# The gated recurrence issued step by step among the chunks of the masked cross attention

## The chip, the cores and the metric

The kernel runs on one core of one Trainium2 chip. The metric is the device time of one execution in microseconds (us). Before the change three runs took 3279.47, 3282.17 and 3289.09 us; the median is 3282.17 us. A difference of 0.3% is about 10 us. Five engines work side by side, each taking its own instructions in the order in which they were issued: PE (matrix products and transposes, with PEld as its weight loads), DVE (vector operations), ACT (activation functions and copies), POOL (elementwise work beside DVE, and the gathers) and SP (which issues most DMAs). The results of PE go to PSUM, here eight buffers ("banks") of 128 x 512 numbers.

## The reference

A decoder of four blocks on 128 sequences of 64 tokens with 128 features. Each of its twelve steps is `x = layernorm(x + step(x))`: attention of some kind, cross attention to a context, and a feed-forward step. The three steps that matter here stand at the end of the third block and the beginning of the fourth:

- `L2_ffn`: a short convolution, a mixture of eight experts, an RMS norm, and a small feed-forward step;
- `L3_attn`: no attention in the usual sense, but a gated recurrence. With `xn` the RMS-normed input, `q, kv, a = split(xn @ W.T)`, the state is `h[t] = sigmoid(a[t]) * h[t-1] + kv[t]`, and the output is `q * h`;
- `L3_xattn`: cross attention with 16 heads of 8 features under a mask that differs for every sequence, query and key.

After them comes `L3_ffn`, a routed mixture of experts (top 1).

## The kernel before

The 8192 tokens are 16 chunks `X[0]` to `X[15]` of 512 tokens (`CT`; 8 sequences), each held in SBUF as 128 partitions x 4 x 128 numbers for the whole run. A list `steps` calls one function per step; the loads of the next step's weights and the functions follow each other, and a scheduler inside the framework fixes the order of instructions on each engine from the program's order and its own estimate of times. `tc.issue_after(ins)` adds an edge of issue order: what is issued inside must stand behind `ins` on its engine.

Buffers come from pools by tag. SBUF tags with their buffer counts are in `SPACES` (`xT`, `qT`, `kT`, `o`, `oT`, `tmp` two each, `r` three). PSUM has `bank()` (three banks) and `wide()` (five banks).

`ffn_conv` works on pairs of chunks in 8 turns. A turn runs eight `units` (one per 128 tokens: expert products, SiLU, weighting, sums), and between them `take` draws steps from two generators: `begin` of the next pair and `end` of the last pair. `end` turns the sums, projects them, computes an RMS norm (`norm`), scales the accumulators (the loop on `h[:, t, :]`), transposes them (`transposed`, L325), and runs the small feed-forward step (products `dn`, a GELU, products `u`). The last pair's `end` runs by itself after the eighth turn, then a last layer norm.

`attn_scan` is the recurrence. For each chunk: squares on ACT, their sum and a reciprocal square root on DVE (`rsqrt`, eleven small dependent operations, L340 to L345), scaling to `xn` half on POOL and half on ACT, four transposes, three products of 512 columns (q, kv, gate), a sigmoid on ACT, the scan on DVE (L1807), a product with q, four transposes back, the residual sum, and the layer norm of the result. It runs as a software pipeline in which chunk i is normed while chunk i-4 gets its layer norm. No other step's work stands beside it, except where one step's end meets the next one's beginning.

`xattn_masked` calls `mha`, the loop that all attention steps share. One iteration c of it holds, in program order: `weights(c, 0)` (products `t_ps` in four wide banks, then four exponentials `e`), the load and transposes of chunk c+2, `values(c-1, 1)`, `scores(c+1, 0)` (products `s_ps` in four wide banks, then four maxima L1183 on DVE), the output transposes of chunk c-1, `project_v(c+1)`, `weights(c, 1)`, `values(c, 0)`, `scores(c+1, 1)`, `project(c+2)` with the eight head-masked copies `eb`, the output product, `maxima(c+1)` (a transpose `mT_ps` on PE and its copy `mT`, L1202) and the layer norm of chunk c-1. The loop goes from c = -2 to 16. A callback `aside(c, k, seen)` is called four times in each iteration, k = 0 to 3, with instructions behind which its work shall stand; `xattn_masked` passes `kept`, which from c = 2 on draws steps of the next step's routing.

The layer norm of a chunk ends on POOL in `ln_apply` (L380, four operations) up to chunk 11, and on ACT (L378) beyond.

Of the kernel before, what the change touches and what calls it, by code (L numbers as in the profile page):

```python
# [12 lines left out]
F32 = mybir.dt.float32  # L13
# [4 lines left out]
ALU = mybir.AluOpType  # L18
# [216 lines left out]
def tile_decoder(ctx: ExitStack, tc: tile.TileContext, a, out):  # L235
# [1245 lines left out]
    def xattn_masked():  # L1481
        w = W[10]

        rows_of = a["amask"], a["amaskT"]
        store = {}
        begin = cross(w, "l3xbq", "l3xbk")

        used = BPC * 8 * 18

        def prepare(c, s):  # L1490
            m = work("t1", (P, BPC * 2 * S // 4), "mu").bitcast(U8), VX[c % 2][:, used + 512 : used + 768].bitcast(U8)
            for x, src in zip(m, rows_of):
                for g in range(4):
                    nc.sync.dma_start(out=x[32 * g : 32 * g + 32], in_=src[c])
            then = begin(c, s)

            def step(n):
                f = (work("ye", (P, 512), "mf") if n == 0 else VX[c % 2][:, used : used + 512]).bitcast(BF16)
                V.tensor_scalar(f, m[n], 0.0, NEG, ALU.is_equal, ALU.mult)
                store[c, n] = f.rearrange("p (b n k) -> p b n k", b=BPC, n=2)  # L1500
                return then(n)

            return step

        def mask(c, hf, s, t):
            for h in range(2):
                for x in range(2):
                    for g in range(4):
                        if s:
                            f = rows32(store[c, 0], g)[:, 4 * hf + x : 4 * hf + 4 : 2, h, None, :].to_broadcast([32, 2, 4, S])  # L1510
                            mm(
                                s[g][x * S : (x + 1) * S].rearrange("p (u h k) -> p u h k", u=2, h=4), rows32(idh, g)[:, h, :], f,
                                start=False, stop=(h == 1), skip_group_check=True,
                            )
                            continue
                        f = rows32(store[c, 1], g)[:, None, 4 * hf : 4 * hf + 4, h, :].to_broadcast([32, 2, 4, S])
                        mm(t[g][x * S : (x + 1) * S], rows32(idh, g)[:, h, :], f, start=False, stop=False, skip_group_check=True)

        mha(
            prepare, w[:, 2, :],  # L1520
            lambda c, s: out_projected(c, s["o"], w[:, 3, :], bv=col("l3xbv"), base=lambda: with_bias(c, "l3xbo"), on_act=c > 11),
            mask=mask, aside=kept,
        )


# [76 lines left out]
    def ffn_conv():  # L1602
# [83 lines left out]
        def end(i):  # L1686
# [27 lines left out]
            for n in pair:  # L1714
                h = acc[n]
                for t in range(TPC):
                    V.scalar_tensor_tensor(h[:, t, :], h[:, t, :], y[:, 0, n, t : t + 1], row("normw"), ALU.mult, ALU.mult)  # L1717
                hT.append(transposed(h, "oT"))
                b = with_bias(2 * i + n, "upb")
                G.tensor_tensor(b, b, h, ALU.add)  # L1720
                base.append(b)
                yield
# [27 lines left out]
        def take(it, n=1):  # L1750
            for _ in range(n):
                next(it, None)
# [5 lines left out]
        for i in range(turns):  # L1758
            b = begin(i + 1) if i + 1 < turns else none
            e = end(i - 1) if i else none  # L1760
            for g in range(8):
                units(i, g // TPC, g % TPC)
                if g == 0:
                    take(tail)
                    take(b, 2)
                elif g == 1:
                    take(e, 2)
                elif g == 2:
                    take(b, 2)
                elif g == 3:  # L1770
                    take(e, 3)
                elif g == 4:
                    take(b, 2)
                elif g == 5:
                    take(b)
                elif g == 6:
                    take(e, 2)
                elif g == 7:
                    take(e)
            tail = e  # L1780
        take(tail)
        for _ in end(turns - 1):
            pass
        v = sm.tile([P, 2, 2, TPC], F32, tag="cv", name="cv")
        G.memset(v[:, 0], 1.0)
        norm(v, turns - 1, S_[turns - 1])
# [1 line left out]


    def attn_scan():  # L1790
        w = W[9]
        xs, hs, rs = {}, {}, {}
        kept = work("h", (P, 8, 512), "scan")

        def project(c):
            xT = transposed(xs.pop(c), "xT", scale=col("gamma"))
            q = bank("q_ps")
            mm(q, w[:, 0, :], xT, start=True, stop=True)
            ps = [wide("kva_ps") for _ in range(2)]
            for k in range(2):  # L1800
                mm(ps[1 - k], w[:, 2 - k, :], xT, start=True, stop=True)
            g = work("qT", name="gate")
            A.activation(g, ps[1], AF.Sigmoid)

            G.memset(g.rearrange("p (b s) -> p b s", b=BPC)[:, :, 0:1], 0.0)
            h = hs[c] = kept[:, c % 8]
            V.tensor_tensor_scan(h, g, ps[0], 0.0, ALU.mult, ALU.add)  # L1807
            V.tensor_tensor(h, h, q, ALU.mult)

        def recalled(c):  # L1810
            h = hs.pop(c)
            y = bank("y")
            for t in range(TPC):
                q = slice(t * P, (t + 1) * P)
                nc.tensor.transpose(y[:, q], h[:, q], ident)
            r = rs[c] = work("r", (P, TPC, D))
            V.tensor_tensor(r, y.rearrange("p (t d) -> p t d", t=TPC), X[c], ALU.add)

        def squares(c):
            s = xs[c] = work("tmp", (P, TPC, D), "sq")  # L1820
            A.activation(s, X[c], AF.Square)


        squares(0)
        for i in range(NC + 4):
            v = sm.tile([P, 2, TPC], F32, tag="lnv2", name="lnv2")
            a_, b_ = i, i - 4
            if a_ < NC:
                V.tensor_reduce(v[:, 0], xs[a_], AX.X, ALU.add)
                V.tensor_scalar(v[:, 0], v[:, 0], 1e-24, None, ALU.max)  # L1830
            else:
                G.memset(v[:, 0], 1.0)
            if b_ >= 0:
                r = rs.pop(b_)
                mv = ln_stats(r, v[:, 1])
            else:
                G.memset(v[:, 1], 1.0)
            if a_ + 1 < NC:
                squares(a_ + 1)
            y = rsqrt(v.rearrange("p n t -> p (n t)"), 2 * TPC, "rms")  # L1840
            if a_ < NC:
                V.tensor_scalar(y[:, :TPC], y[:, :TPC], math.sqrt(D), None, ALU.mult)
                xn = xs[a_] = work("o", (P, TPC, D), "xn")
                for t in range(TPC):
                    if t % 2:
                        A.activation(xn[:, t, :], X[a_][:, t, :], AF.Identity, scale=y[:, t : t + 1])
                    else:
                        G.tensor_scalar(xn[:, t, :], X[a_][:, t, :], y[:, t : t + 1], None, ALU.mult)
            if b_ >= 0:
                ln_apply(b_, r, mv, y[:, TPC:], on_act=True)  # L1850
            if 0 <= i - 3 < NC:
                recalled(i - 3)
            if 0 <= i - 1 < NC:
                project(i - 1)


    n_rows = [(len(cs) * CT + E8 * (GR - 1)) // GR * GR for cs in SWITCH_BATCHES]
# [25 lines left out]
    def ffn_switch():  # L1883
# [5 lines left out]

    steps = [  # L1890
        moe_top2, xattn_single, ffn_ternary, attn_diff, xattn_causal, ffn_routed,
        attn_alibi, xattn_padded, ffn_conv, attn_scan, xattn_masked, ffn_switch,
    ]
    seen = None
    for n, step in enumerate(steps):
        load_weights(n + 1)

        with tc.issue_after(seen) if seen else nullcontext():
            seen = step()
# [16 lines left out]
```

## Time and profile before

| | us |
|---|---|
| median of three runs | 3282.17 |
| the profiled execution | 3278.03 |
| its span on the core | 3276.3 |
| the conv's last turn ends (last `units` on DVE) | 2545 |
| first product of the recurrence (q) | 2586 |
| first transposes of the masked attention | 2689.7 |
| its first `weights` (L1213) | 2710.1 |
| one iteration of its loop (start of `scores` to the next) | 18.95 |

In the page, part 1 gives the busy time of each engine, part 2 the same in 40 slices of some 82 us each. A table of windows gives the busy time in stated stretches, and the timeline lists instructions in order of time: start, duration, engine, line, operation, output from input, count, and in square brackets the idle time before it with what ended it. Where several instructions are merged in one line, the duration is that of the whole group.

### The profile page before, as it was taken

The numbers are of one execution on the slowest core, as the hardware profiler recorded it, in microseconds if no ns is written. First come the engines' busy times: TensorE is split into PE (matmuls) and PEld (weight loads), VectorE is DVE, ScalarE is ACT, GpSimd is POOL, SyncE is SP. The second block draws the span as 40 slices with busy tenths as digits, with TensorE's granted clock in tenths as the row PEclk, the third lists the DMA queues.
The fourth block names the chain that finished last, engine by engine and source line by source line (L and its number), as shares of the span: only waits on it lengthen the run. The fifth ranks groups of instructions, "written<-read, shape, count | busy, mean of one in ns | idle before, by whom it ended". The sixth has DMA issues, their size and how long they took to land. (4 is left out here: it accounts for less than half of the span.)

```text
span 3276.3 us, 110323 instructions
## 1 busy us (share of the span) xinstructions
PE 2882.3 (88%) x47184; PEld 2115.1 (65%) x47184; DVE 1973.2 (60%) x7074; ACT 1614.1 (49%) x3106; POOL 1521.4 (46%) x1548
## 2 busy tenths in 40 slices
PE   5999967999987999999999989998888569998993
PEld 3888834666665777766677767774444336776793
DVE  3733267557777666433256656666778886666246
ACT  3544457445543565333355545643444555654553
POOL 4477473454555344311234445556566322446154
PEclk9999988999998999999999989989988789998997
DMA  5578710000002000000000000000000000001684
GB/s 142 160 214 248 220 52 28 8 1 3 3 3 76 19 4 4 6 1 1 5 11 4 4 5 4 4 13 1 1 1 2 9 1 16 18 15 46 181 266 147
DMA packets 142459, 159.23 MB, mean 49 GB/s; under 512 B 16720, under 2 KB 118096, under 8 KB 141968
## 3 DMA queue, kind: packets, MB, share of 16 engines
q1 hardware_dynamic: 128064, 123.65, 12.7%
q0 software_dynamic: 13184, 27.03, 3.2%
q8 instruction: 370, 6.06, 0.7%
q10 hardware_dynamic: 720, 1.50, 0.1%
q14 instruction: 121, 0.99, 0.1%
HBM read 121.44 MB, written 30.67 MB: 46 GB/s over the span
## 5 line engine op out<-in xcount | busy, mean ns | idle before, releaser
L1183 DVE TENSOR_REDUCE m<-s_ps 128x8 f32<-128x512 f32 x640 | 397.5, 683 | 144.4 <-PE s_ps L1411 50.8
L1232 ACT ACTIVATE e<-t_ps 128x512 f32<-128x512 f32 x640 | 330.0, 601 | 150.7 <-PE t_ps L1225 150.2
L380 POOL TENSOR_SCALAR x<-xb,lnmv,ln_y 128x128 f32<-128x128 f32 x304 | 238.6, 797 | 267.5 <-DVE ln_y L345 267.5
L1250 PE MATMUL av_ps<-vx,e 128*64 128x18 f32 (+1 forms) x10240 | 341.3, 216 | 5.6 <-issue 5.3
L1250 PEld LDWEIGHTS av_ps<-vx,e 128*64 128x64 f32 x10240 | 322.9, 140 | 25.9 <-issue 18.7
L1127 POOL TENSOR_SCALAR eb<-qT,small 128x512 f32<-128x512 f32 x80 | 131.2, 1640 | 431.5 <-ACT qT L943 200.9
L774 ACT ACTIVATE hT<-h_ps,aux 128x256 f32<-128x256 f32 x496 | 206.6, 470 | 208.4 <-PE h_ps L772 102.3
L1213 PE MATMUL t_ps<-eb,kT 32*64 32x128 f32 x10240 | 281.3, 285 | 4.4 <-DVE m L1183 2.2
L805 POOL DMA_INDIRECT got<-l_rout,pli x192 | 194.4, 1012 | 148.7 <-issue 57.7
L772 PE MATMUL h_ps<-ebT,rw 128*128 128x256 f32 x992 | 241.2, 387 | 8.6 <-DMA rw<-in_l0w_dram 4.5
L785 PEld LDWEIGHTS yg<-rw,hT 128*128 128x128 f32 x1984 | 241.8, 192 | 6.4
L1213 PEld LDWEIGHTS t_ps<-eb,kT 32*64 32x64 f32 x10240 | 198.1, 132 | 71.1 <-DVE m L1183 25.6
L785 PE MATMUL yg<-rw,hT 128*128 128x128 f32 x1984 | 242.1, 276 | 0.0
L1175 PE MATMUL s_ps<-eb,qT 32*64 32x256 f32 x5120 | 217.5, 399 | 20.8 <-POOL eb L1127 9.8
L786 DVE TENSOR_TENSOR yo<-yg,aux 128x256 f32<-128x256 f32 x124 | 52.6, 424 | 267.5 <-PE yg L785 264.4
L1255 DVE RECIPROCAL rc<-av_ps 128x32 f32<-128x32 f32 (+1 forms) x192 | 61.7, 321 | 240.7 <-PE av_ps L1250 240.3
L772 PEld LDWEIGHTS h_ps<-ebT,rw 128*128 128x128 f32 x992 | 182.8, 194 | 31.1 <-DVE ebT L760 6.3
L747 POOL DMA_INDIRECT aux<-in_x_dram,plt x156 | 159.9, 1025 | 56.9 <-issue 26.8
L1125 ACT ACTIVATE eb<-qT,small 128x512 f32<-128x512 f32 x160 | 106.8, 715 | 129.3 <-POOL qT L1352 124.1
L380 POOL TENSOR_SCALAR x<-r,lnmv,ln_y 128x128 f32<-128x128 f32 x68 | 54.4, 813 | 225.0 <-DVE ln_y L345 225.0
L1127 POOL TENSOR_SCALAR eb<-kT,small 128x512 f32<-128x512 f32 x80 | 145.9, 1823 | 22.1 <-ACT kT L945 11.3
L1175 PEld LDWEIGHTS s_ps<-eb,qT 32*64 32x64 f32 x5120 | 114.3, 134 | 60.2 <-issue 15.2
(429 smaller groups left out, 6414.5 us busy)
## 6 DMA issues: line engine op xcount, KB each, us to landing
rw<-in_l0w_dram SPq DMA_DIRECT2D x78, 512.0 KB
rw<-in_l3w_dram SPq DMA_DIRECT2D x46, 512.0 KB
l_rout<-yo SPq DMA_DIRECT2D x124, 128.0 KB
aux<-xd SPq DMA_DIRECT2D x46, 128.0 KB
aux<-in_l0b_dram SPq DMA_DIRECT2D x78, 66.0 KB
xd<-vx SPq DMA_DIRECT2D x5, 1024.0 KB
x<-in_x_dram SPq DMA_DIRECT2D x16, 256.0 KB
cin<-in_ctx_dram SPq DMA_DIRECT2D x16, 256.0 KB
```

The lines of the kernel that those rows point to most:

```text
L380: G.tensor_scalar(X[c][:, t, :], r[:, t, :], mv[:, t, 0:1], y[:, t : t + 1], ALU.subtract, ALU.mult)
L747: s.gather = G.indirect_dma_start(out=eb[:, i, :], out_offset=None, in_=x[:, :], in_offset=bass.IndirectOffsetOnAxis(ap=tokens[:, 2 * g + ...
L772: s.pe = mm(ps[:, j * GR : (j + 1) * GR], w1[:, (k + j) * P : (k + j + 1) * P], ebT, start=True, stop=True)
L774: s.act_ins = A.activation(hT[k + j], ps[:, j * GR : (j + 1) * GR], s.act, bias=v[:, k + j : k + j + 1])
L785: s.pe = mm(y[:, i * P : (i + 1) * P], hT[k][:, i * P : (i + 1) * P], w2[:, k, :], start=(k == 0), stop=(k == FK - 1))
L805: s.gather = G.indirect_dma_start(out=got[i][k][:, t, :], out_offset=None, in_=s.rout[b][:, :], in_offset=bass.IndirectOffsetOnAxis(ap=whe ...
L1127: ins = (G if h == 2 else V).tensor_scalar(dst, x, mine, None, ALU.mult)
L1175: mm(ps[g][j * S : (j + 1) * S, u * 256 : (u + 1) * 256].rearrange("p (h k) -> p h k", h=4), rows32(s["q"], g)[:, b], rows32(s["eb"], g)[: ...
L1183: last = V.tensor_reduce(s["m"][:, g, 2 * hf : 2 * hf + 2, :].rearrange("p t h -> p (t h)"), ps[g].rearrange("p (n k) -> p n k", k=S), AX. ...
L1213: mm(ps[g][i * S : (i + 1) * S].rearrange("p (a u j q) -> p a u j q", u=2, a=2, j=2)[:, :, u, j, :], rows32(s["k"], g)[:, b], rows32(s["eb ...
L1232: last = A.activation(e[:, g, :], ps[g], AF.Exp, scale=scale)
L1250: mm(av[j * S : (j + 1) * S, 8 * (u - u0) + n, :], ev[:, n // 2, n % 2, u, j, :], vx[:, 2 * (2 * hf + u) + j, n, :], start=True, stop=True,)
```

## The change

`attn_scan` becomes a generator of four steps for each chunk c, and it is no longer an entry of `steps` (a `None` stands there). The four steps are: (A) the sum of squares, the reciprocal square root for chunk c together with the layer norm of chunk c-1, and the scaling to `xn`; (B) the four transposes and the copy with gamma; (C) the three products, the sigmoid, the scan and the product with q; (D) the transposes back, the residual sum, now in place in `X[c]`, and the squares of chunk c+1. In C all three products now take `bank()` banks; before, two of them took `wide()` ones.

The steps are drawn in three places. In the conv's eighth turn four of them come after `units` 0, 3, 5 and 7. Five more come between the steps of the last pair's `end`. The rest come in `mha`, one at every `aside` call (`recurrent` calls `kept` first and then draws a step under the edges that it was given). So iteration c holds B, C and D of chunk c+4, and A of chunk c+5; the layer norm of the last recurrence chunk falls into iteration c = 11. `prepare` asserts that a chunk has its layer norm before the attention loads it. The buffer tags of the recurrence are other ones in the conv (`tmp`, `kT`, `qT`) than in the attention (`o`, `xT`, `oT`, `r`).

In `end` of the conv the scaling loop is a step of its own now, drawn after `units` 4 by a new `take(e)`, where it was part of the step drawn after `units` 6.

```diff
@@ xattn_masked
+        scan_tags.update({"x": "o", "xT": "xT", "gate": "oT", "h": "r"})
         def prepare(c, s):
+            assert c in scanned
...
-            mask=mask, aside=kept,
+            mask=mask, aside=recurrent,
@@ ffn_conv, end
                 for t in range(TPC):
                     V.scalar_tensor_tensor(h[:, t, :], h[:, t, :], y[:, 0, n, t : t + 1], row("normw"), ALU.mult, ALU.mult)
+            yield
+            for n in pair:
+                h = acc[n]
                 hT.append(transposed(h, "oT"))
@@ ffn_conv, the turns
                 elif g == 4:
+                    take(e)
                     take(b, 2)
...
+                if i == turns - 1 and g in (0, 3, 5, 7):
+                    take(scan)
             tail = e
         take(tail)
-        for _ in end(turns - 1):
-            pass
+        for n, _ in enumerate(end(turns - 1)):
+            take(scan, n % 2)
@@ attn_scan, now a generator
+        squares(0)
+        for c in range(NC + 1):
+            v = sm.tile([P, 2, TPC], F32, tag="lnv2", name="lnv2")
+            if c < NC:
+                V.tensor_reduce(v[:, 0], xs[c], AX.X, ALU.add)
+                V.tensor_scalar(v[:, 0], v[:, 0], 1e-24, None, ALU.max)
...
+            if c:
+                mv = ln_stats(X[c - 1], v[:, 1])
...
+            y = rsqrt(v.rearrange("p n t -> p (n t)"), 2 * TPC, "rms")
+            if c < NC:
+                V.tensor_scalar(y[:, :TPC], y[:, :TPC], math.sqrt(D), None, ALU.mult)
+                xn = xs.pop(c)
+                for t in range(TPC):
+                    if t % 2:
+                        A.activation(xn[:, t, :], X[c][:, t, :], AF.Identity, scale=y[:, t : t + 1])
+                    else:
+                        G.tensor_scalar(xn[:, t, :], X[c][:, t, :], y[:, t : t + 1], None, ALU.mult)
+            if c:
+                ln_apply(c - 1, X[c - 1], mv, y[:, TPC:], on_act=True)
+                scanned.add(c - 1)
+            yield
+            if c == NC:
+                return
+            ps = bank("xT_ps")
+            for t in range(TPC):
+                nc.tensor.transpose(ps[:, t * P : (t + 1) * P], xn[:, t, :], ident)
+            xT = work(scan_tags["xT"], name="xT")
+            A.activation(xT, ps, AF.Identity, scale=col("gamma"))
+            yield
+            w = W[9]
+            kv, ps, q = (bank(n) for n in ("kv_ps", "gate_ps", "q_ps"))
+            for n, d in (2, ps), (1, kv), (0, q):
+                mm(d, w[:, n, :], xT, start=True, stop=True)
+            g = work(scan_tags["gate"], name="gate")
+            A.activation(g, ps, AF.Sigmoid)
+            V.memset(g.rearrange("p (b s) -> p b s", b=BPC)[:, :, 0:1], 0.0)
+            h = work(scan_tags["h"], name="scan")
+            V.tensor_tensor_scan(h, g, kv, 0.0, ALU.mult, ALU.add)
             V.tensor_tensor(h, h, q, ALU.mult)
+            yield
             y = bank("y")
             for t in range(TPC):
                 q = slice(t * P, (t + 1) * P)
                 nc.tensor.transpose(y[:, q], h[:, q], ident)
+            added(c, y, X[c])
+            if c + 1 < NC:
+                squares(c + 1)
+            yield
+
+    def recurrent(c, k, seen):
+        kept(c, k, seen)
+        with ExitStack() as behind:
+            for i in seen:
+                if i:
+                    behind.enter_context(tc.issue_after(i))
+            next(scan, None)
```

More of the change, by code (lines that the diff above doesn't have):

```diff
@@ L1790, in attn_scan @@
     def attn_scan():
[L1791 to L1807, printed above, removed]
+        xs = {}
@@ new lines, in squares @@
+        def squares(c):
+            s = xs[c] = work(scan_tags["x"], (P, TPC, D), "sq")
+            A.activation(s, X[c], AF.Square)
+        squares(0)
[5 more added lines that the diff above has]
+            else:
+                G.memset(v[:, 0], 1.0)
+            if c:
+                mv = ln_stats(X[c - 1], v[:, 1])
+            else:
+                G.memset(v[:, 1], 1.0)
+            y = rsqrt(v.rearrange("p n t -> p (n t)"), 2 * TPC, "rms")
[5 more added lines that the diff above has]
+                        A.activation(xn[:, t, :], X[c][:, t, :], AF.Identity, scale=y[:, t : t + 1])
+                    else:
+                        G.tensor_scalar(xn[:, t, :], X[c][:, t, :], y[:, t : t + 1], None, ALU.mult)
[20 more added lines that the diff above has]
+            V.tensor_tensor_scan(h, g, kv, 0.0, ALU.mult, ALU.add)
@@ L1808, in project @@
             V.tensor_tensor(h, h, q, ALU.mult)
-        def recalled(c):
-            h = hs.pop(c)
+            yield
             y = bank("y")
@@ L1815, in recalled @@
                 nc.tensor.transpose(y[:, q], h[:, q], ident)
[L1816 to L1854, printed above, removed]
+            added(c, y, X[c])
+            if c + 1 < NC:
+                squares(c + 1)
+            yield
+    scanned = set()
+    scan_tags = {"x": "tmp", "xT": "kT", "gate": "qT", "h": "tmp"}
+    scan = attn_scan()
+    def recurrent(c, k, seen):
[5 more added lines that the diff above has]
+            next(scan, None)
     n_rows = [(len(cs) * CT + E8 * (GR - 1)) // GR * GR for cs in SWITCH_BATCHES]
@@ L1891, in tile_decoder @@
         moe_top2, xattn_single, ffn_ternary, attn_diff, xattn_causal, ffn_routed,
-        attn_alibi, xattn_padded, ffn_conv, attn_scan, xattn_masked, ffn_switch,
+        attn_alibi, xattn_padded, ffn_conv, None, xattn_masked, ffn_switch,
     ]
@@ L1896, in tile_decoder @@
         load_weights(n + 1)
+        if step is None:
+            continue
         with tc.issue_after(seen) if seen else nullcontext():
```

## The prediction

> **What bounds the kernel now.** I read the page first, then a table of windows over the stretch that the change touches, then the timeline of that stretch, engine by engine.
>
> ```profile
> span 3276.3 us, 110323 instructions
> PE 2882.3 (88%) x47184; PEld 2115.1 (65%) x47184; DVE 1973.2 (60%) x7074; ACT 1614.1 (49%) x3106; POOL 1521.4 (46%) x1548
> ...
> PEclk9999988999998999999999989989988789998997
> ```
> ```profile
> 2577.00:2690.00 113.00, 74.17 (x249) 38.09 (x250) 97.83 (x437) 61.15 (x140) 23.70 (x54) 0.88 0.00 1
> 2690.00:2712.00 22.00, 12.90 (x179) 7.43 (x177) 14.69 (x56) 13.22 (x26) 8.61 (x7) 0.84 0.00 1
> 2712.00:2865.00 153.00, 146.35 (x4101) 111.29 (x4102) 98.87 (x297) 93.62 (x163) 55.79 (x47) 0.99 0.07 18
> ```
>
> The columns of a window are its length, busy PE, PEld, DVE, ACT and POOL, granted clock, DMA share and GB/s. PE bounds the kernel on the whole. In the recurrence (first row) DVE is busy 87% and PE waits; in the masked attention (third row) PE is busy 96% at full clock, while DVE has 35% and ACT 39% free. The change moves the first kind of work into the second. So the recurrence's stretch falls away, and the question is what each attention iteration grows by. That is read from one iteration, engine by engine:
>
> ```profile
> 2789.76 1.12 PE L1175 MATMUL s_ps<-eb,qT 32*64 32x256 f32 x32
> 2804.41 0.23 PE L1200 MATMUL mT_ps<-identh,hl 128*128 128x128 bf16 x1 [0.41 <-DVE hl L1194]
> 2806.14 0.66 PE L325 MATMUL xT_ps<-ident,x 128*128 128x128 f32 x4
> ```
> ```profile
> 2785.93 0.22 DVE L1202 COPY mT<-mT_ps 128x128 bf16<-128x128 bf16 x1
> 2786.84 0.36 DVE L368 BATCH_NORM_AGGREGATE lnmv<-lnst 128x2 f32<-128x6 f32 x4
> 2790.08 0.16 DVE L345 SCALAR_TENSOR_TENSOR ln_y<-ln_u,ln_y 128x4 f32<-128x4 f32 x1
> ...
> 2790.35 3.12 POOL L380 TENSOR_SCALAR x<-xb,lnmv,ln_y 128x128 f32<-128x128 f32 x4 [2.90 <-DVE ln_y L345]
> ```
>
> PE starts `s_ps` 3.83 us after DVE copied `mT` (2785.93 to 2789.76), with hardly a gap. The layer norm on DVE and POOL needs until 2793.47, 7.5 us after `mT`, and nobody on PE waits for it.
>
> **The change part by part.** The sum is made against the profiled execution, 3278.0 us (span 3276.3 and 1.7 around it), which lies 4.1 under the median.
>
> *Products and transposes.* Rows of one chunk in the recurrence:
>
> ```profile
> 2591.71 1.13 PE q_ps L1798 x2
> 2592.84 1.73 PE kva_ps L1801 x4
> ...
> 2654.46 2.07 PE q_ps L1798 x2
> ```
>
> The chain of waits gives 2.86 us for the six matmuls at full clock; less the last one's tail, 0.43 each, 2.6. The two groups of four transposes start 0.44 apart (2594.39 to 2594.83). So a chunk costs PE 0.44 + 2.6 + 0.44 = 3.5. Nothing hides that, as PE is full. Chunks 4 to 15 run in iterations 0 to 11: 12 x 3.46 = **+41.5**. Chunks 0 to 3 run in the seam, counted below.
>
> *A stall of PE before `scores`.* Step A of chunk c+5 is issued behind `mT`, and step B's transposes stand on PE in front of the next iteration's `s_ps` in the built order. PE has 3.83 us of own work between `mT` and `s_ps`, 4.27 with B. On DVE, after `mT`, stand the layer norm as before, a reduction (0.60), four statistics and the other small ones. Interleaved with the old chain they put the final `ln_y` at 5.15 (4.15 before) and the recurrence's `rms_y` 1.7 later, at 6.85 (eight dependent operations, 0.2 apart). POOL has L380 ahead of its half of `xn`: 5.25 + 3.12 + two of 0.60 = 9.57; the transposes of the last tiles end at 9.9. On ACT two of the four exponentials of `weights` stand behind `xn` and the layer norm of chunk c+4. These rows price them:
>
> ```profile
> 2601.39 1.19 POOL L1848 TENSOR_SCALAR xn<-x,rms_y 128x128 f32<-128x128 f32 x2 [0.51 <-DVE lnv L1830]
> 2601.71 0.68 ACT L1846 ACTIVATE xn<-x,rms_y 128x128 f32<-128x128 f32 x2
> 2602.30 1.63 ACT L378 ACTIVATE x<-r,lns,rms_y 128x128 f32<-128x128 f32 x4
> ```
>
> 6.85 + 0.7 + 1.65 + 0.55 = 9.8 until the third exponential frees the fourth wide bank for `s_ps`. Both ways end at 9.9 against 4.27: 5.6 of stall in each of ten iterations (A of chunks 6 to 15). Behind the stopped PE wait `s_ps`, then DVE's maxima and the whole iteration. Where L380 is absent (A of chunks 4 and 5), DVE's chain is 4.45 and the ACT way gives 7.3: 3.1 each. A's last call (iteration 11) has only the ACT way, about 5. Sum 56 + 6 + 5 = **+67**. Ends: 4.5 each if the small operations fill each other's gaps better, 7.5 if L380 takes 3.69, as it does at 2968.75, and `xn` 0.72, as at 2577.14: 54 to 88.
>
> *PE's clock after the stalls.* These rows show a start after 7.34 us of idle time, to set against the 1.12 us row above:
>
> ```profile
> 2701.89 2.01 PE L1175 MATMUL s_ps<-eb,qT 32*64 32x256 f32 x32 [7.34 <-ACT eb L1125]
> 2703.62 1.14 PE L1511 MATMUL s_ps<-mf,half 32*64 32x512 bf16 x16
> ```
>
> The mask's 16 take 0.64 in the steady loop. So a long idle time costs some 1.4 us afterwards; idle times of about 3 us in the recurrence mostly cost nothing (only some q products take 2.07 for 1.13). 5.6 lies between: 0 to 2.5 each, I take 1.5, ten times: **+15** (0 to 25).
>
> The page "TensorE: Matmul & The Clock Gate" of the Trainium skill, section "Part 1: The HAM clock gate", says that an idle window of about 3.4 us halves the clock until a busy window has passed. By it a 5.6 us stall contains such a window in about two cases of three, and the term would be some 11. The 2.01 us row agrees with the halving; nothing here shows the window's length.
>
> *Sigmoids among exponentials.* ACT's built order has a table load before every sigmoid and another after it:
>
> ```profile
> L1803 ACT ACT_TABLE_LOAD x1 | 1.3, 1283 | 0.0
> ```
>
> Two of 1.28 and the sigmoid (0.60) follow the copies of `v_ps`, which end 1.3 after `project_v`; the exponentials are free to start 4.5 after it. PE has the three products (2.6) and `weights` (2.15) until then, 4.7. So the cover is 0.2 us: I count 0, and if it is gone the cost is what exceeds it, up to 2.6 each, 31 in all. The three `bank` banks are held until the scan and the product with q end, 8.3 after `s_ps` began; the next users want them at 7.9, 10.1 and 11.1, and the first takes the gate's, free at 6.3. Zero. Per chunk ACT adds 6.2 us (61.15 over 17 in the first window, and 2.6 of loads) to its 11.6, and DVE 5.8 (97.83 over 17) to its 12.3, in some 28 us: neither binds. SP and the gathers are not moved.
>
> The page "ScalarE: Activation LUTs", section "What ACT_TABLE_LOAD costs", gives a switch 2.66 us, drain included, where the row has 1.28 and shows no drain. By it the two loads would take 2.8 more than I count, the cover of 0.2 is gone, and 12 iterations cost 31: the upper end of this term.
>
> *The seam.* Before, the attention's first transposes come at 2689.7 and its first `weights` at 2710.1. After, the conv's end goes on to it directly. In the conv's end now, the early squares and roots of chunks 1 to 3 hold up ACT and DVE (the GELU of 2559.75 waits behind a square that waits for DVE); without them, and with the scaling ahead of the last units, turn 6's `u` and the last sums come some 9 us sooner (2553 for 2562). A to D of chunk 1 cost DVE about 4 of that back. I put `u` of the last pair at 2575 (2582 before), the attention's first transposes at 2577. From there to `weights` took 20.5; chunk 2's products, sigmoid, scan and transposes now stand before q and k on PE, 6 us more: 2603. **-107** (97 to 113, as little of this overlap is to be read off a row).
>
> *The scaling in the conv.* Before, the eight scalings alternate with the routing's small operations, and PE waits:
>
> ```profile
> 2425.70 0.95 PE L325 MATMUL oT_ps<-ident,acc 128*128 128x128 f32 x2 [3.21 <-DVE acc L1717]
> 2432.83 1.79 PE L1725 MATMUL dn_ps<-oT,cols 128*32 128x512 f32 x4
> ```
>
> After, they stand together: eight of 0.34 and one blocked by POOL for a further 1.0 end near 2428.4, two expert products follow, and `dn` comes at 2430.0, 2.8 sooner. The routing's chain is put behind the scalings, which can take it all back. Six turns of 0 to 2.7: I take 1.3, **-8** (0 to 16).
>
> Sum: 41.5 + 67 + 15 + 0 - 107 - 8 = +8.5, and 2 for iteration 11, where eight routing steps fall beside the recurrence's end: +10.5. 3288.5 on the profiled execution's scale, **3293** on that of the median.
>
> **The rivals.** (1) *Slower by more:* the table loads come onto PE's path, since the cover is 0.2 us. +31: 3324; at two thirds of it 3314. For it: ACT's order is fixed and copies, loads and sigmoid are serial there. Against: only three of the four wide banks' exponentials are wanted early. (2) *No change:* the seam and the growth cancel; +8.5 is inside their ends. It takes only the clock term at 0: 3278. (3) *Faster, the other side:* step A's chain costs PE little, because DVE gets through the two interleaved chains sooner than PE reaches the transposes. It decides at an iteration period of some 28.5 us: 115 saved over 12 iterations are 9.6, onto 18.95. At a stall of 3.1 in all (the ACT way without L380) growth is 41.5 + 37 and no clock loss: -36, 3246. At no stall, which speaks for the change doing just what it says, -73: 3209. Against both: the 7.5 us that the old layer norm already takes after `mT`.
>
> **How the numbers follow.** Forecast (3292 to 3314) 0.35; rival 1 (beyond) 0.12; rival 2 (3272 to 3292, within 0.3%, about what the three runs can tell from no change) 0.22; rival 3 0.31, of which no stall at all 0.06. Slower 0.47, same 0.22, faster 0.31. The added ends (-113 - 16 + 41.5 + 54 = -33.5, and -97 + 41.5 + 88 + 25 + 2 = +59.5) give 3249 to 3342. With 0.1 beyond on each side the range is 3248 to 3322. The forecast's own range is 3280 to 3314.
>
> **What would show it.** Right: iterations 1 to 10 last 28 to 30 us; PE idles 5 to 6 before the recurrence's transposes, released by POOL `xn`; the first `weights` starts near 2600; `s_ps` after a stall takes up to 2.0. Wrong: a period under 27 or over 31, the stall before `av_ps` or `s_ps` released by ACT's sigmoid or exponentials, or the first `weights` after 2615 or before 2590.

## The result and the profile after

The changed kernel takes 3332.5 us (median of four runs, 3327.45 to 3335.51) beside 3284.2 us for the kernel before (four runs): the ratio is 1.0145, with a 95% interval of 1.0125 to 1.0166. It is slower by 48 us; the forecast was 3293, its range 3248 to 3322.

The page of the changed kernel:

```profile
span 3331.2 us, 110218 instructions
PE 2920.1 (88%) x47184; PEld 2125.1 (64%) x47184; DVE 1963.1 (59%) x7057; ACT 1648.4 (49%) x3134; POOL 1518.9 (46%) x1526
...
PEclk9999978999998999999999989998888788898997
```

PE has the same 47184 instructions as before and is busy 37.8 us longer with them: its clock was lower. The windows (columns as in the prediction; the first two of after, the third of before) show where:

```profile
2497.60:2627.85 130.25, 101.08 (x497) 52.49 (x495) 105.22 (x308) 68.69 (x130) 59.66 (x59) 0.84 0.02 7
2715.55:2958.86 243.31, 200.49 (x4172) 136.49 (x4173) 143.60 (x546) 144.43 (x249) 72.00 (x72) 0.87 0.04 11
```
```profile
2766.71:2916.66 149.95, 146.08 (x4060) 110.74 (x4060) 101.83 (x321) 92.69 (x161) 62.77 (x57) 1.00 0.07 18
```

The first row goes from the convolution's last `pw` products to the attention's first `weights`; before, the same stretch took 224.7 us. The second holds eight iterations of the attention, the third the same eight before: 30.41 us each where they took 18.74, a clock of 0.87 where it was 1.00, and PE idle for 43 of 243 us where it was idle for 4 of 150. The table of waits, PE in the attention, names the one who ended that idle time (us in total, times, longest):

```profile
PE xT_ps L1837 <- POOL sq L1828: 49.9, 11, 5.0
PE mT_ps L1200 <- DVE hl L1194: 6.6, 11, 1.5
PE lg_ps L539 <- DVE o L1264: 2.6, 1, 2.6
```

L1837 are the recurrence's transposes (step B), L1828 is POOL's half of `xn` (step A; the buffer is called `sq`). One iteration on PE, from `mT_ps` on:

```profile
2805.63 0.23 PE L1200 MATMUL mT_ps<-identh,hl 128*128 128x128 bf16 x1 [0.41 <-DVE hl L1194]
...
2807.94 2.05 PE L1250 MATMUL av_ps<-vx,e 128*64 128x18 f32 x64
2814.88 1.27 PE L1837 MATMUL xT_ps<-ident,sq 128*128 128x128 f32 x4 [4.89 <-POOL sq L1828]
2816.07 2.02 PE L1175 MATMUL s_ps<-eb,qT 32*64 32x256 f32 x32
2817.84 1.11 PE L1514 MATMUL s_ps<-mf,half 32*64 32x512 bf16 x16
...
2821.15 1.13 PE L1844 MATMUL gate_ps<-xT,w_l3a 128*128 128x512 f32 x2
```

PE stands 4.89 us before the transposes, and then needs 2.02 us for the `scores` products that took 1.12 before. The chain that it waits for, on DVE and POOL:

```profile
2809.15 0.25 DVE L368 BATCH_NORM_AGGREGATE lnmv<-lnst 128x2 f32<-128x6 f32 x2
2812.61 0.17 DVE L1822 TENSOR_SCALAR rms_y<-rms_y 128x4 f32<-128x4 f32 x1
2811.11 3.12 POOL L380 TENSOR_SCALAR x<-xb,lnmv,ln_y 128x128 f32<-128x128 f32 x4 [3.61 <-DVE rms_u L344]
2814.22 1.18 POOL L1828 TENSOR_SCALAR sq<-x,rms_y 128x128 f32<-128x128 f32 x2
```

`rms_y` is done at 2812.78, 6.8 us after `mT` was copied (at 2805.99); POOL scales only when L380 is through, and the transposes follow.

The two profiled executions differ by 54.9 us of span, in three stretches:

| stretch | before | after | difference | forecast |
|---|---|---|---|---|
| start to the `pw` of the conv's eighth turn | 2485.36 | 2497.60 | +12.2 | -8 |
| from there to the attention's first `weights` | 224.7 | 130.25 | -94.5 | -107 |
| from there to the end | 566.2 | 703.35 | +137.2 | +125.5 |

Of the +12.2, 4.9 had arisen before the conv's second turn, where the code is unchanged.

### The profile page after: what moved, and what is told of

The parts are those of the page before. It is cut to its first block, busy times and chain, and to the rows that moved or that the text cites. A ratio compares the mean times of both kernels' runs of the same rounds, so it can differ in the third digit from the quotient of the medians.

```text
span 3331.2 us, 110218 instructions
## 1 busy us (share of the span) xinstructions
PE 2920.1 (88%) x47184; PEld 2125.1 (64%) x47184; DVE 1963.1 (59%) x7057; ACT 1648.4 (49%) x3134; POOL 1518.9 (46%) x1526
## 5 line engine op out<-in xcount | busy, mean ns | idle before, releaser
L380 POOL TENSOR_SCALAR x<-xb,lnmv,ln_y 128x128 f32<-128x128 f32 x304 | 238.8, 797 | 276.2 <-DVE ln_y L345 234.1
L1175 PE MATMUL s_ps<-eb,qT 32*64 32x256 f32 x5120 | 237.9, 419 | 13.5 <-POOL eb L1127 10.5
L1125 ACT ACTIVATE eb<-qT,small 128x512 f32<-128x512 f32 x160 | 106.8, 715 | 129.7 <-POOL qT L1352 125.4
L380 POOL TENSOR_SCALAR x<-r,lnmv,ln_y 128x128 f32<-128x128 f32 x68 | 54.8, 818 | 225.0 <-DVE ln_y L345 225.0
```

The source lines that it names most:

```text
L380: G.tensor_scalar(X[c][:, t, :], r[:, t, :], mv[:, t, 0:1], y[:, t : t + 1], ALU.subtract, ALU.mult)
L1175: mm(ps[g][j * S : (j + 1) * S, u * 256 : (u + 1) * 256].rearrange("p (h k) -> p h k", h=4), rows32(s["q"], g)[:, b], rows32(s["eb"], g)[: ...
```

## The experiments

The theory after reading: the growth of an iteration is PE's own 3.5 us, plus the stall before step B, plus PE's clock after that stall; both of the latter come from *where* the steps stand, not from their work. Rivals: the work added on DVE and ACT (5.8 and 6.2 us an iteration by the prediction) sets the period; the table loads do; the conv's scaling costs time.

The runs came in three sets, each with its own runs of the kernel before. In the first two sets that took some 3520 us: the conv's second turn began some 140 to 160 us later there, and the part behind the attention was longer too, while the old attention's iterations took 18.85 us, nearly as elsewhere. So ratios within a set are compared, and the length of an iteration (mean of eight, from the fourth `mT_ps` to the twelfth). The steps in the conv's end are counted with the four in its eighth turn. All results:

| run | steps in the conv's end | iteration, us | ratio to before (95%) |
|---|---|---|---|
| before | - | 18.74 | 1 |
| the change | 9 | 30.41 | 1.0145 (1.0125 to 1.0166) |
| the change again, third set | 9 | 30.40 | 1.0123 (1.0092 to 1.0155) |
| before, scaling sooner | - | 18.85 | 1.0002 (0.9988 to 1.0015) |
| the change, scaling at its old place | 8 | 25.00 | 0.9943 (0.9929 to 0.9957) |
| eight steps | 8 | 25.00 | 0.9968 (0.9955 to 0.9981) |
| seven steps | 7 | 27.46 | 1.0075 (1.0051 to 1.0100) |
| six steps | 6 | 28.54 | 1.0125 (1.0099 to 1.0151) |
| five steps | 5 | 34.38 | 1.0337 (1.0316 to 1.0359) |
| all of `xn` off POOL | 9 | 30.81 | 1.0124 (1.0100 to 1.0148) |
| no table loads | 9 | 30.28 | 1.0115 (1.0096 to 1.0134) |
| PE filled in the stall | 9 | 28.28 (seven) | 1.0097 (1.0077 to 1.0117) |
| `xn` a chunk ahead | 9 | 25.44 | 0.9944 (0.9925 to 0.9963) |
| steps placed anew | 8 | 22.34 | 0.9859 (0.9838 to 0.9881) |

**The scaling alone, and taken back.**

```diff
@@ first run, on the kernel before; the second takes the same lines out of the changed one
                     V.scalar_tensor_tensor(h[:, t, :], h[:, t, :], y[:, 0, n, t : t + 1], row("normw"), ALU.mult, ALU.mult)
+            yield
+            for n in pair:
+                h = acc[n]
                 hT.append(transposed(h, "oT"))
...
                 elif g == 4:
+                    take(e)
                     take(b, 2)
```

> The kernel before with the conv's scaling a step sooner, nothing else changed. By the forecast's term (-8, ends 0 and -16) it is faster than before: 3268 to 3284, 3276 likeliest. Rival, from the trace of after, whose turns in the conv are 0.8 to 2.2 us longer than those of before in six of seven cases: the scaling itself costs, +7, 3291 (the turn's transposes still wait for the last scaling, and the units behind it on DVE come later).

Ratio 1.0002 (0.9988 to 1.0015): neither the forecast's -8 nor the +7 read from the trace of after; both lie outside the interval (-4 to +5 us). The products `dn` do not come sooner: over the six turns they stand 32.4 to 36.8 us after the turn's `pw` before, and 32.7 to 39.0 after; in the turn that the prediction had read it is 35.8 before and 36.0 after (2408.46 to 2444.49). DVE's scalings in that turn, first the end of the group of before, then the group of after:

```profile
2428.55 1.88 DVE L1717 SCALAR_TENSOR_TENSOR acc<-acc,rms_y,rows 128x128 f32<-128x128 f32 x3
```
```profile
2435.66 4.96 DVE L1720 SCALAR_TENSOR_TENSOR acc<-acc,rms_y,rows 128x128 f32<-128x128 f32 x8
```

The eight in a row take 4.96 where the forecast had 3.7. They end 1.2 us sooner than the spread ones (32.2 after `pw`, 33.4 before), and four expert products at half clock (3.62 us) take that back in front of `dn`.

> The changed kernel with the scaling back at its old place (after units 6); the recurrence's steps stay where they are. By the forecast's term it is 8 us slower than the changed kernel, 3340. By the rival it is 7 us faster, 3325, and the turns of the conv go back to 37.5, 45.3, 40.9, 45.1 and 44.1 us.

0.9943: some 20 us faster than before. But this run changed two things, and the expectation says otherwise: the edit took a `yield` out of `end`, so `take(scan, n % 2)` drew four steps there and not five. Eight steps in all, and every later step fell one aside later. An iteration took 25.0 us. The next runs take the number of steps by itself.

**The number of steps in the conv's end.** The attention draws a step at each of its four asides, so this number sets which step stands at which aside.

```diff
-            take(scan, n % 2)
+            take(scan, n % 2 and n < 8)   # eight steps; n < 6: seven; n < 4: six; n < 2: five
```

> The changed kernel with eight steps of the recurrence drawn in the conv's end and not nine (the scaling stays a step sooner). Every later step then falls one aside later: A at k = 0 behind the exponentials, B at k = 1 behind the first maxima, C at 2, D at 3. If the place of B in front of scores makes the growth, an iteration takes 25 us as in the run with the scaling at its old place (which had also lost one step in the conv's end), twelve of them save some 62, and the ratio to before is 0.993 to 0.997. If it was the scaling that made the difference there, the ratio stays near 1.0145.

0.9968 and 25.00 us: the place theory holds. No wait for `xn` is left in the iterations; PE waits for two smaller things (waits of PE, us, times, longest):

```profile
PE mT_ps L1200 <- DVE hl L1194: 14.8, 12, 1.5
PE oT_ps L325 <- DVE o L1264: 9.0, 9, 1.2
```

Between this run and the last there is only the early scaling: 0.25%, with intervals that touch. Taken with the run of the scaling alone, it costs something between nothing and some 10 us, and wins nothing.

> The same with seven steps: A at k = 1 behind the first maxima, B at 2 behind values, C at 3 behind mT, D at 0. A's chain on DVE (5.5 us) then starts behind the maxima; PE has project_v, weights and values in the meantime, some 5.7. Place theory: a stall of 2 to 3 us before B, a period near 26 to 27, ratio 0.999 to 1.004. If the place of the steps does not matter, 1.0145.

1.0075, 27.46 us: more than expected. The wait for `xn` is 9.4 us in four places only; in its stead `scores` waits 11.3 us for exponentials that stand behind the recurrence's `xn` and layer norm on ACT, and `av_ps` 8.7 us behind the recurrence's three products (perhaps for a bank; the trace names a small DVE operation there).

> The same with six steps: A at k = 2 behind values(c, 0), B at 3 behind mT, C at 0, D at 1. A's chain on DVE then stands before the second maxima, so mT comes late and PE waits at its transpose. Place theory: 3 to 4 us of wait there, none before B, a period near 26 to 27, ratio 0.999 to 1.005. If the place does not matter, 1.0145.

1.0125, 28.54 us: slower than the place theory had it, and by the ratio alone not to be told from 1.0145; the iteration and the waits tell the two apart. There is a wait at `mT_ps`, as expected, but of 1.9 us and not 3 to 4, ended by the copies `eb` on ACT; a second one stands at `t_ps`, and the clock was 0.90 over the eight iterations. None for `xn` is left (waits of PE, us, times, longest):

```profile
PE mT_ps L1200 <- ACT eb L1125: 17.3, 9, 1.9
PE t_ps L1213 <- DVE m L1183: 12.6, 29, 2.0
```

> The changed kernel with five steps in the conv's end and not nine; the places in the attention's iterations stay, one chunk later. The seam loses one chunk's steps (products 2.6, transposes 0.9 and their waits, some 8 to 12 us by the trace of after), one more iteration carries a chunk (+11). If the seam's steps lie on its path as read, the two cancel: ratio 1.012 to 1.016. If they were hidden there, it is 8 to 11 us slower than the changed kernel, 1.017 to 1.018.

1.0337, 34.38 us: far off. Here a step keeps its aside, one chunk later. The seam is 129.7 us to the first `mT_ps` where the change has 132.6, so four steps fewer give 3 us, not 8 to 12. What the expectation overlooked is the lead: with nine steps a chunk gets its layer norm an iteration before the attention loads it, with five it gets it just before:

```profile
2831.84 0.47 PE L325 MATMUL xT_ps<-ident,x 128*128 128x128 f32 x1 [4.69 <-ACT x L378]
```
```profile
PE xT_ps L325 <- ACT x L378: 49.3, 11, 4.8
```

The same chain makes a stall of about the same length; it only ends in another wait. The iteration is 4 us longer than the change's all the same: PE is busy for 29.2 us of it and not 25.1, at a clock of 0.84 and not 0.87. Where that comes from, no run takes apart.

**What is behind the stall: POOL alone?**

```diff
-                        G.tensor_scalar(xn[:, t, :], X[c][:, t, :], y[:, t : t + 1], None, ALU.mult)
+                        V.tensor_scalar(xn[:, t, :], X[c][:, t, :], y[:, t : t + 1], None, ALU.mult)
```

> The half of the scaling to xn that POOL does goes to DVE, so that it no longer stands behind L380. If POOL's way alone holds up PE, the transposes of the recurrence start when ACT's half of xn ends, 1.4 us sooner in each of ten iterations: -14, with some of the clock loss 3310 to 3318. If, as the prediction had it, ACT's way (xn, layer norm, then the third exponential, which frees the fourth wide bank) ends at the same time, the transposes come sooner but scores then waits for that bank: the stall moves behind the transposes, and the gain is 0 to 6 us, 3326 to 3332.

1.0124, an iteration of 30.8: nothing gained. The transposes do come sooner, but `scores` stops at the third exponential, which ACT makes behind its part of `xn` and the layer norm:

```profile
2994.97 1.12 PE L1837 MATMUL xT_ps<-ident,sq 128*128 128x128 f32 x4 [3.37 <-DVE sq L1828]
2996.02 2.02 PE L1175 MATMUL s_ps<-eb,qT 32*64 32x256 f32 x21
...
3000.06 1.12 PE L325 MATMUL oT_ps<-ident,o 128*128 128x128 f32 x4
```
```profile
2996.68 1.05 ACT L1232 ACTIVATE e<-t_ps 128x512 f32<-128x512 f32 x2
```

The output's transposes come 12.8 us after `mT_ps` (2987.24), where the change has 13.25: both ways end together, as the prediction had worked out.

**PE's clock after the stall.**

```diff
             ps = bank("xT_ps")
+            for t in range(32 if c > 5 else 0):
+                nc.tensor.transpose(ps[:, t % 4 * P : (t % 4 + 1) * P], ident, ident)
             for t in range(TPC):
```

> The changed kernel with 32 transposes of the identity in front of the recurrence's own four (chunks 6 to 15), into the same bank, which the four then overwrite: 4.7 us of PE work in the stall of 4.9, everything else in the same order. If the time lost after a stall is PE's clock (2.7 us an iteration in the trace of after), it goes: an iteration takes 27.8 and not 30.5, ten of them save 25 to 30, ratio 1.005 to 1.008. If the matmuls after a stall are slow for another reason (operands, banks), nothing is saved: 1.014.

1.0097, beside 1.0123 for the change in the same set; an iteration takes 28.28 and not 30.40. The chain is as long as it was (4.9 us from the end of `av_ps` to the transposes; the fillers cover 3.7 of it), and PE runs on at full speed. In windows, the stall and the time after it: the change, then this run:

```profile
2809.93:2814.88 4.95, 0.06 (x4) 0.01 (x1) 3.35 (x22) 2.07 (x6) 3.77 (x6) 0.86 0.11 28
2814.88:2818.00 3.12, 3.12 (x44) 1.86 (x50) 0.00 (x0) 2.18 (x5) 1.77 (x2) 0.50 0.00 0
```
```profile
2801.06:2806.01 4.95, 3.71 (x36) 3.47 (x32) 3.35 (x22) 2.06 (x6) 3.76 (x6) 1.00 0.11 28
2806.01:2812.88 6.87, 6.72 (x94) 3.79 (x94) 2.48 (x4) 5.48 (x10) 1.79 (x2) 1.00 0.01 2
```

So the clock is shown as the cause of 2.1 us an iteration; the trace of after gives 2.5 (6.27 us from the transposes to the recurrence's products, where the same work takes 3.73 in the run with the steps placed anew, below). The whole saving is only 7 to 9 us: in iteration 11, where no stall had been, the fillers are pure cost (36.4 us for 31.9), and in iteration 10 a stretch of 10.4 us ran at a clock of 0.51 with only 0.64 us of idle time before it. Why is not settled.

**Table loads.**

```diff
-            A.activation(g, ps, AF.Sigmoid)
+            A.activation(g, ps, AF.Identity, scale=0.01)
```

> The changed kernel with the sigmoid replaced by a scaled copy on the same engine (the gate is then not the reference's), so that none of the table loads around it is needed. By the forecast the loads lie beside weights on PE and cost nothing: ratio 1.012 to 1.0145. By the first rival they are on PE's path: 14 to 31 us less than the changed kernel, ratio 1.005 to 1.010.

1.0115, an iteration of 30.28 and not 30.40; iterations 0 to 11 take 361.0 us, where the change takes 360.4 and 357.9 in its two profiles. So the loads cost next to nothing, where the first rival has 14 to 31 us. The ratio is less sharp, as the change itself was not run in this set: it is 0.8 thousandths under the change's ratio in the third set, 3 under that in the first. ACT then waits for `t_ps` all the longer:

```profile
2994.61 2.07 ACT L1232 ACTIVATE e<-t_ps 128x512 f32<-128x512 f32 x4 [2.77 <-PE t_ps L1225]
```

2.77 is about the two loads (2.57) and the 0.18 that ACT waits there in the change.

**`xn` made a chunk ahead.** The core of the edit; the squares go two chunks ahead, in buffers that are free at that time. `late` holds in the attention: there the roots are all that stands in A, and `xn` of chunk c + 1, the layer norm and the transposes of chunk c stand in B.

```diff
@@ step A, for chunk c
-                V.tensor_reduce(v[:, 0], xs[c], AX.X, ALU.add)
...
+            roots = [(0, 0), (1, 1)] if c == 0 else [(0, c + 1)] if c + 1 < NC else []
+            for n, k in roots:
+                V.tensor_reduce(v[:, n], xs[k], AX.X, ALU.add)
...
+            late = "late" in scan_tags
+            if late:
+                yield
+            for n, k in roots:
+                xn = xs[k]
...
             if c:
                 ln_apply(c - 1, X[c - 1], mv, y[:, TPC:], on_act=True)
                 scanned.add(c - 1)
-            yield
+            if not late:
+                yield
```

> The scaling to xn is made one chunk ahead (the squares two ahead), and in the attention the scaling and the layer norm of the last chunk stand in step B behind the exponentials, not in step A. So the transposes of the recurrence find xn ready, and nothing of step A stands in front of the exponentials. If the stall and the lower clock after it make up the growth beyond the products, an iteration goes from 30.5 to 23 to 24 us, ten of them save 65 to 75, and the kernel takes 3257 to 3267, faster than before. If the growth is in the work of DVE and ACT or in the banks instead, a period stays above 27 and the time above 3300.

0.9944: faster than before, the stall is gone, the clock is whole. But an iteration is 25.4 us, not 23 to 24:

```profile
2913.34 0.66 PE L1845 MATMUL xT_ps<-ident,ctx 128*128 128x128 f32 x4
2917.14 0.63 PE L325 MATMUL oT_ps<-ident,o 128*128 128x128 f32 x4 [1.67 <-DVE o L1264]
```

A's chain still stands on DVE in front of `o`, which the output's transposes want (15.4 us of waits in nine iterations).

**All steps placed by what waits for them.**

```diff
@@ the generator in the attention; its four steps are drawn at k = 0, 1, 2 and 3
+        for c in range(2, NC):
+            xT = turned(c)
+            yield
+            h = scanning(xT)
+            ks = (c + 1,) if c + 1 < NC else ()
+            done = roots(ks, c - 1)
+            yield
+            applied(ks, c - 1, *done)
+            yield
+            recalled(c, h)
+            yield
...
@@ mha
-                weights(c, 1)
+                exps = weights(c, 1)
...
-            aside(c, 2, (behind, spread))
+            aside(c, 2, (behind, spread, exps if c in on else None))
```

> The recurrence between the chunks of the attention with its steps put elsewhere: the transposes of chunk c (k = 0) use an xn made in the iteration before; products, sigmoid and scan at k = 1; the sums of squares, layer-norm statistics and roots behind the first maxima at k = 1; scaling to xn and layer norm behind the second four exponentials at k = 2; transposes back at k = 3. Eight steps in the conv's end, the conv's scaling at its old place. If only the place of the steps made the growth, an iteration takes 18.95 plus the 3.5 to 4 of PE's own work, 22.5 to 23, and the seam gives 94: 45 to 50 us faster than before, ratio 0.986 to 0.988. If the work added on DVE and ACT sets a period of its own, it stays at 25 and the ratio at 0.994.

3241.5 us where before takes 3289.1 in the same set: 0.9859 (0.9838 to 0.9881), 48 us faster, as the place theory had it. Eight of its iterations, and one on PE:

```profile
2686.32:2865.01 178.69, 174.37 (x4173) 124.40 (x4173) 150.07 (x545) 143.20 (x246) 76.07 (x72) 1.00 0.06 15
```
```profile
2757.85 0.66 PE L1834 MATMUL xT_ps<-ident,ctx 128*128 128x128 f32 x4
2758.43 1.12 PE L1175 MATMUL s_ps<-eb,qT 32*64 32x256 f32 x32
...
2761.58 1.13 PE L1843 MATMUL gate_ps<-xT,w_l3a 128*128 128x512 f32 x2
```

DVE and ACT carry the same work as in the change (150 and 143 us, there 144 and 144), in 179 us where that took 243, and PE is busy 98% at full clock. So neither DVE nor ACT had set the period. This run also has the conv's scaling at its old place, but so has the run at 0.9943, so that does not explain the gain.

**The change itself once more.**

> The changed kernel as it is, on the chip of these runs, where the kernel before takes some 3520 us. The difference of 48 to 55 us should be the same: ratio 1.0135 to 1.0155.

1.0123 (1.0092 to 1.0155), 3328.4 us beside 3289.1 (not the 3520 that was expected for this set): +39, a little under the band, with iterations as in the first profile. The change costs 39 to 48 us.

## Why the prediction was right or wrong

The direction was the likeliest case, and its mechanism is what the trace shows: step A's chain holds up PE in front of step B, at the place, with the releaser and nearly at the length that was worked out. The size was not: 39 to 48 us and not 10.5, outside the range. One of its own signs of being wrong came, a first `weights` after 2615 (2627.85). Three terms failed: the clock after the stalls was taken at half its price, the waits of step A's chain were left out in the seam, and the gain of the scaling did not come. A fourth, the stall, was too large, and hid most of the clock's error by luck.

Iterations 0 to 11, which hold the recurrence's chunks 4 to 15, in three windows: before, after, and the run with the steps placed anew, which has the same products as after:

```profile
2712.47:2940.59 228.12, 218.44 (x5993) 163.92 (x5994) 148.67 (x446) 138.16 (x239) 85.75 (x75) 0.99 0.07 18
2630.17:2990.52 360.35, 300.16 (x6160) 201.61 (x6161) 215.03 (x782) 215.53 (x370) 103.88 (x103) 0.87 0.04 11
2620.88:2893.69 272.81, 263.42 (x6160) 186.74 (x6160) 220.27 (x778) 213.19 (x365) 106.75 (x100) 0.98 0.06 15
```

After, PE is idle for 60 us of them (10 before), and busy for 36.7 us more than in the run with the same products. By the prediction's own steps:

- *Products and transposes, +41.5.* Right. With all stalls gone an iteration grows by 3.60 (22.34 against 18.74), 43 in twelve.
- *The stall, +67.* Too large by 17: 49.9 in eleven waits, nine of 4.9 to 5.0 and, with chunks 4 and 5, 3.9 and 1.9 (3.1 each was forecast). In the steady iterations it is 4.9 and not 5.6; `rms_y` came 6.8 after `mT`, as worked out, but PE's own work lasted 4.0 and not 3.8, and the transposes began 8.9 after `mT`, when POOL's `xn` was only half done. The last B, in iteration 11, did not wait (2.6 came in front of another step), nor did `scores` after A's last call, for which 5 stood. (By the terms given, the ends of the sum are 56 and 86, not 54 and 88.) That ACT's way is equally long was right: with POOL's part away the wait moved to the third exponential.
- *The clock, +15.* Too small by half: some 31 in all, the 36.7 us above less 6 for the split products below. A steady iteration loses 2.1 (by the filled run) to 2.5 (by the trace) and not 1.5. Every stall of 4.9 was followed by 3 to 6 us at 0.50, and the two short ones, priced at nothing here, by 13.4 and 6.7 us. The page "TensorE: Matmul & The Clock Gate" of the Trainium skill, section "Part 1: The HAM clock gate", puts the idle window at about 3.4 us, and the prediction worked out a term of 11 from it; in these rows not two thirds of the stalls but all are followed by the halved clock, and one after 1.89 us is too.
- *A cost that was not in the sum.* In six iterations D's transposes stand between the sixth and the seventh of the second `scores` products: `s_ps`, mask and `y` take 3.06 us (2829.29 to 2832.35), where 1.48 and 0.58 would be expected. That is 1 us each, about 6 in all.
- *Table loads, 0.* Right; rival 1's time of 3314 to 3324 was near, its mechanism is refuted. The Trainium skill's price of 2.66 us for a switch ("ScalarE: Activation LUTs", "What ACT_TABLE_LOAD costs") does not show here: the trace has 1.28 for each load, and without them ACT waits 2.77 where it waited 0.18.
- *The seam, -107.* Measured -94.5. Two steps of it failed. `u` of the last pair was to come 7 us sooner; counted from the last `pw` it came 1.7 sooner (94.9 for 96.6), though turn 6's `u` was 7.1 sooner (forecast 9). And from the first transposes to the first `weights` the prediction added 6 us of PE's work to 20.5; it was 34.3. In the run with the steps placed anew the same stretch takes 26.2 (2588.03 to 2614.27), just what the forecast had. So the missing 8 us are of the size of the waits in the recurrence's steps (1.5 and 5.2 for POOL's `xn` before the transposes, 1.3 each before products and transposes back), which are of the kind that the prediction had priced in the iterations and left out in the seam. What keeps the conv's end long is not settled: with four steps fewer `u` still came 93.3 after `pw`.
- *The scaling, -8.* Wrong: 0, by the run that makes this edit alone. The step that failed is that the eight scalings end at 2428.4, 3.7 us after they begin (they took 4.96 in a row), and that `dn` comes 2.8 sooner. A small cost is likelier than nothing, though within that run's interval: from the conv's second turn to its eighth, the eleven traces with the scaling sooner take 261.8 to 266.3 us, the three with it at its old place 257.1 to 261.5.
- *The sum.* Of the 44 us between forecast and profile, 12 are the attention's: the clock (16 more) and the split products (6) less the stall (17), and some 7 in smaller terms, 3 of them behind iteration 11. 12 are the seam's, and 8 the scaling's gain that did not come. The other 12 arose before the conv's eighth turn, 5 of them before its second, where the code is unchanged; the second measurement of the change, +39 and not +48, shows how much of such a sum can be chance. The result lies within the ends added up (3249 to 3342) but outside the narrower range: the seam and the scaling came out beyond and at the unfavourable ends of their own ranges (-94.5 for -97 to -113, 0 for 0 to -16), and the 12 us in the conv had no term.

Rival 3 asked the right question, the period at which the change breaks even, and put it at some 28.5 us. In the runs, 27.46 gives 1.0075 and 25.0 gives 0.994 to 0.997, so it lies near 26. Its case without a stall is the run with the steps placed anew, which gained 48 us where the rival had 73.

## What to carry to other kernels

When a serial chain is cut into steps and drawn between the iterations of a loop whose bottleneck engine is full, ask for each step which engine's next instruction stands behind it, and how much own work that engine has until the chain's end; a chain of 7 to 9 us in front of 4 us of work is a stall in every iteration, and moving the same steps by one slot was worth some 15 to 70 us (ratios 1.0145, 0.9968, 1.0075, 1.0125 and 1.0337 for nine to five steps). Give such a chain a whole iteration of lead, and tie its parts on the other engines behind what is wanted sooner. And price the stalls of the steady loop also in the stretch that leads up to it.

## What the runs showed of the hardware that was not expected

PE's clock after idle time, over the waits of four traces (before, the change, seven steps, `xn` ahead) between the conv's last turn and the end of the attention: after 3.8 us or more, sixteen of sixteen waits at full clock were followed by 0.50 to 0.62 for the next 3 us; between 1.9 and 3.5 us some were and some were not (1.89: 0.50, 2.21: 1.00, 3.02: 1.00, 3.10: 0.50); waits of 1.7 us and less in the steady loop nearly all went on at 1.00. An idle time of 4.9 us thus costs 4.9 and then 2.1 to 2.5. Work did not always bring the clock back soon: after the wait of 3.9 in the change's trace, PE was busy without a gap from 2636.19 to 2649.60, all of it at 0.50. And there are stretches of some 10 us at half clock with no such idle time ahead of them (0.51 from 2930.9 to 2941.3 in the run with PE filled), whose cause stays open.
